# Other places in the steps for parts of a chunk's fronts and ends, in a two-layer kernel (selective scan, then outlook attention)

## The chip, the cores and the metric

The kernel runs on one core of a Trainium2 chip. What is measured is the device time of one execution in microseconds. Five engines work side by side, each through its own instruction stream in order: TensorE (PE; its weight loads are listed as PEld), VectorE (DVE), ScalarE (ACT), GpSimd (POOL), and SyncE (SP), which here only issues transfers (DMAs).

## The reference, cut to what matters

Input `x` has shape (4, 384, 64, 64); all data are float32. Two residual layers follow each other, each on a group norm of its input. The change concerns the first, a selective state-space layer over L = 4096 positions with 768 inner channels and 16 states:

```python
xn = (xs - mu) * jax.lax.rsqrt(var + 1e-05) * ln_w + ln_b
xz = jnp.einsum('blc,dc->bld', xn, in_proj_w)
xb, z = jnp.split(xz, 2, axis=-1)
xc = _silu(conv(xb, conv_w) + conv_b)            # 4 taps, one filter per channel
x_dbl = jnp.einsum('bld,ed->ble', xc, x_proj_w)  # 24 columns dt, 16 B, 16 C
dt = softplus(jnp.einsum('blr,dr->bld', dt, dt_w) + dt_b)
def step(h, inp):
    dA = jnp.exp(dt_t[:, :, None] * A[None])
    h = dA * h + (dt_t * x_t)[:, :, None] * B_t[:, None, :]
    y_t = jnp.einsum('bdn,bn->bd', h, C_t)
y = (ys + xc * D) * _silu(z)
out = jnp.einsum('bld,cd->blc', y, out_proj_w)
```

(The convolution's call and the loop over positions are shortened here.) The second layer, an outlook attention with 3 x 3 windows, is not touched.

## The kernel before, in words

**Tiling.** The 4096 positions of each of the four images are cut into 17 chunks of TM = 241, so there are 68 chunks. A chunk's scan takes NU = 12 steps; a step is one "unit" of 64 channels with all 16 states, which are laid on partitions and in four groups. The loop at line 805 runs over steps `s`; `s` modulo 12 is the place of a step in the chunk that is being scanned.

**The scan of a unit** is spread over several steps. `s_inputs` (line 625, POOL) and `s_inputs2` (line 640, DVE) multiply `dxr` with B into a buffer `h`, half of the groups each; `s_decay` (line 649, ACT) computes exp(dt A) into `da` in PSUM, four instructions for each half unit; `s_scan` (line 661, DVE) does the recurrence, twice per unit; `s_outputs` (line 671, POOL) multiplies by C; `s_sum` (line 676, PE), at odd steps, adds the states of two units up into `y`; `s_gate` (line 694, DVE) applies the gate. `h` has five buffers, so at an odd step the buffer for unit `s + 2` is one that `s_sum` of the same step must have read.

**The fronts and ends.** What comes before a chunk's scan (load, layer norm, in-projection, convolution, silu, the projections to dt, B and C, softplus, and the stores of dt x and dt to DRAM from where they are fetched back in the scan's layout) and what comes after it (out-projection, residual, store) is cut into parts, `f_...` and `e_...`. The dictionaries `plan` (line 505) and `ends` (line 540) give each part a place: a relative step and one of six slots within it, EARLY, READY, SCAN, POOL, MID, LATE. `parts(s, when)` (line 567) runs those that fall due. Relative step `r` of a chunk `k` is `s - 12 (k - 2)`; the chunk's own scan begins at `r = 24`, so parts with `r` from 12 to 23 run beside the scan of the chunk before, at its steps `r - 12`. An end's key counts from 36 later. At one slot the newer chunk's parts come first. `catch_up` (line 556) maps the same table onto the few steps before the second chunk.

**What sets the order.** Every engine is wrapped in `InOrder` (line 34), so its instructions run in the order in which the Python code issues them. A step issues, in this order: fetches (even steps), EARLY, `s_inputs2`, `s_gate` (even steps), READY, the statistics of the next image's input where due, first scan, carry and first decay, save, second scan, SCAN, second decay, `s_outputs`, POOL, `s_inputs`, `s_sum` (odd steps), MID, LATE.

**Buffers.** All tiles `ps_...` of the fronts and ends (and `pm`, `pv`, `pb` of the group norm) share the pool `pmm` with two PSUM buffers: an engine that is to write a new one waits until the last reader of an older one is done. Which of the two is taken is settled when the program is built. `dtx` has two buffers in SBUF, `xr` two.

Parts that the text names: `f_square` (299), `f_pow` (321), `f_rs` (325), `f_scale` (336), `f_x` and `f_z` with `project` (347 to 398), `f_conv` (375), `f_silu` (406), `f_bc` (414), `f_xd` (424), `f_dt` (434), `f_log` (456), `f_spread` (462), `f_plog` (481), `f_dtx` (486), `e_load` (705), `e_project` (710), `e_store` (718).

Of the kernel before, what the change touches and what calls it, by code (L numbers as in the profile page):

```python
# [7 lines left out]
F32 = mybir.dt.float32  # L8
AF = mybir.ActivationFunctionType
# [3 lines left out]
P = 128  # L13
# [7 lines left out]
TM = 241  # L21
# [54 lines left out]
def group_norm_coeffs(pe, ve, ae, gp, small, psum, blk12, mhalf, st, sc, bi):  # L76

    mv = small.tile([P, NCB, 2], F32, tag="mv", name="mv")  # L80
    neg = small.tile([P, 1], F32, tag="mg", name="neg")
    dev = small.tile([P, NCB], F32, tag="dev", name="dev")
    for cb in range(NCB):
        ve.bn_aggr(mv[:, cb, :], st[cb])
    yield False
    ps = psum.tile([P, 2, TM], F32, tag="mm", name="pm")
    for cb in range(NCB):
        pe.matmul(ps[:, 0, 0:1], blk12, mv[:, cb, 0:1], start=(cb == 0), stop=(cb == NCB - 1))
    yield True
    ae.mul(neg, ps[:, 0, 0:1], -1.0)  # L90
    ae.activation(dev, mv[:, :, 0], AF.Square, bias=neg)
    yield False
    ps = psum.tile([P, 2, TM], F32, tag="mm", name="pv")
    for cb in range(NCB):
        pe.matmul(ps[:, 0, 0:1], blk12, mv[:, cb, 1:2], start=(cb == 0), stop=False)
    for cb in range(NCB):
        pe.matmul(ps[:, 0, 0:1], blk12, dev[:, cb : cb + 1], start=False, stop=(cb == NCB - 1))
    yield True
    ve.tensor_scalar_add(sc, ps[:, 0, 0:1], 1e-5)
    gp.tensor_tensor(sc, sc, mhalf[:, 0:1], ALU.pow)  # L100
    yield False
    ae.mul(bi, neg, sc)
# [3 lines left out]
def mamba_layer(ctx, tc, x, w, x1, sc1, bi1, consts, behind):  # L106
# [16 lines left out]
    blk12, ident, eps, one = consts  # L123
    pe, ve, ae, gp, sp = (
        InOrder(tc, e) for e in (nc.tensor, nc.vector, nc.scalar, nc.gpsimd, nc.sync)
    )
# [12 lines left out]
    pmm = ctx.enter_context(tc.tile_pool(name="pmm", bufs=2, space=bass.MemoryType.PSUM))  # L139
# [294 lines left out]
    def f_dt(c, jj):  # L434
        t = c.t
        if jj == 0:
            c.dt = front.tile([P, NJ, TM], F32, tag="dt", name="dt")
        pp = pmm.tile([P, 2, TM], F32, tag="mm", name="ps_dt")
        for h in range(2):
            j = 2 * jj + h  # L440
            pe.matmul(
                pp[:, h, :t], wdt[:, j * P : (j + 1) * P], xd[:, 1:], start=True, stop=True
            )
        ae.activation(c.dt[:, 2 * jj : 2 * jj + 2, :t], pp[:, :, :t], AF.Exp)

    def store(v, d):
        for q in range(4):
            sp.dma_start(d[:, :, q, :].rearrange("j c t -> c j t"), v[CG * q : CG * (q + 1)])
# [31 lines left out]

    def f_plog(c, jj):

        c.pl = pmm.tile([P, 2, TM], F32, tag="mm", name="ps_lg")
        ae.activation(c.pl, c.dt[:, 2 * jj : 2 * jj + 2, :], AF.Ln, bias=one)

    def f_dtx(c, jj):
        if jj == 0:
            c.dxd = dram.tile([NJ, CG, 4, TM], F32, tag="dxd", name="dxd")
        dtx = front.tile([P, 2, TM], F32, tag="dtx", name="dtx", bufs=2)
        ve.tensor_mul(dtx, c.pl, c.xc[:, 2 * jj : 2 * jj + 2, 1:])  # L490
        store(dtx, c.dxd[2 * jj : 2 * jj + 2])


# [2 lines left out]
    EARLY, READY, SCAN, POOL, MID, LATE = range(6)  # L496

    def at(f, *args):
        def part(c):
            f(c, *args)  # L500

        part.f = f
        return part
# [2 lines left out]
        (-12, SCAN): [f_load],  # L506
        (-10, EARLY): [f_mean],
        (-10, READY): [f_center],
        (-9, POOL): [f_square],
        (-7, EARLY): [f_var],  # L510
        (-7, MID): [f_root],
        (-6, SCAN): [f_pow],
        (-5, READY): [f_rs],
        (-5, SCAN): [f_scale],
        (6, MID): [at(f_x, 0)],
        (8, EARLY): [at(f_z, 0)],
        (8, MID): [at(f_x, 1)],
        (9, POOL): [at(f_z, 1)],
        (9, MID): [at(f_conv, 0)],
        (10, LATE): [at(f_z, 2)],  # L520
        (11, LATE): [at(f_x, 2)],
        (12, SCAN): [at(f_conv, 1)],
        (12, LATE): [at(f_conv, 2)],
        (13, POOL): [at(f_silu, "xc", "zs")],
        (14, POOL): [f_bc],
        (15, EARLY): [f_xd],
        (16, READY): [at(f_dt, 0)],
        (16, SCAN): [at(f_dt, 1)],
        (17, EARLY): [at(f_dt, 2)],
        (17, READY): [at(f_plog, 0)],  # L530
        (17, MID): [at(f_dtx, 0)],
        (18, EARLY): [at(f_plog, 1)],
        (18, SCAN): [at(f_dtx, 1), at(f_plog, 2)],
        (19, READY): [at(f_dtx, 2)],
        (19, POOL): [f_log],
        (19, MID): [f_spread],
        (22, SCAN): [f_b],
    }

# [2 lines left out]
        (4, READY): [lambda c: e_project(c, 0)],  # L542
        (6, EARLY): [lambda c: e_project(c, 1)],
        (6, POOL): [lambda c: e_project(c, 2)],
        (15, EARLY): [lambda c: e_store(c)],
    }

    def chunk(k):
# [152 lines left out]
    def e_tokens(c, v):  # L701

        return v[c.b, :, c.t0 - 1 + c.lo : c.t0 - 1 + TM].rearrange("(p cb) l -> p cb l", cb=NCB)
# [6 lines left out]
    def e_project(c, cb):  # L710
        lo = c.lo
        po = pmm.tile([P, 2, TM], F32, tag="mm", name="ps_out")
        pe.matmul(po[:, 0, lo:], ident, c.xr[:, cb, lo:TM], start=True, stop=False)
        for j in range(NJ):
            pe.matmul(po[:, 0, lo:], wout[:, j, cb, :], c.zs[:, j, lo:TM], start=False, stop=(j == NJ - 1))
        ae.copy(c.xr[:, cb, lo:TM], po[:, 0, lo:])

    def e_store(c):
        if c.ci == 0:
            st1[c.b] = small.tile([P, NCB, NC, 6], F32, tag="st1", name="st1")  # L720
        for cb in range(NCB):
            ve.bn_stats(st1[c.b][:, cb, c.ci, :], c.xr[:, cb, c.lo : TM])
        sp.dma_start(e_tokens(c, x1), c.xr[:, :, c.lo : TM])
        if c.ci == NC - 1:
            b = c.b
            st = [st1[b][:, cb].rearrange("p a s -> p (a s)") for cb in range(NCB)]
            made = group_norm_coeffs(
                pe, ve, ae, gp, small, pmm, blk12, mhalf, st, sc1[:, b : b + 1], bi1[:, b : b + 1]
            )
            norms.append([made, False])  # L730
# [509 lines left out]
def layers(ctx, tc, w, out):  # L1240
# [26 lines left out]

    started = []
    mamba_layer(tc, x.rearrange("b c h w -> b c (h w)"), w, x1, sc1, bi1, consts, behind)
    outlook_layer(tc, x1, w, out, sc1, bi1, weights, ready)  # L1270

# [68 lines left out]
```

## Time and profile before

| | |
|---|---|
| time, median of 3 runs | 6282.82 us (6279.14 to 6284.06) |
| the profiled execution's own time | 6275.31 us |
| its span, first to last instruction | 6273.5 us |
| granted TensorE clock, mean | 0.94 |
| busy: PE, DVE, ACT, POOL | 88%, 86%, 74%, 85% of the span |
| first layer's scans | about 115 to 5036 us of the span |

The page cuts the span into 40 slices of about 157 us; slices 2 to 32 are the first layer, the rest the second. A row of the groups gives line, engine, operation, what is written from what, shapes and count, then busy time in us and mean ns of one, then the engine's idle time just before and what ended it. Nearly every instruction has line 49, that of the helper which keeps the order, so groups are told apart by the names of their tiles. In the timeline a row is start and length in us, engine and instruction, and in brackets the idle time before it with its releaser. A wait for several things is put down to the one that came last.

### The profile page before, as it was taken

How to read it: one execution, taken by the hardware profiler on the slowest of the kernel's cores; microseconds unless marked ns; L12 is line 12 of the kernel's file. 1: busy time of each engine (PE TensorE's matmuls, PEld its weight loads, DVE VectorE, ACT ScalarE, POOL GpSimd, SP SyncE). 2: the span in 40 equal slices, each digit the busy share in tenths (PEclk: the TensorE clock that was granted, in tenths of full speed). 3: DMA queues.
4: the chain of work that ended last, by engine and by line, in shares of the span. 5: the costliest groups of instructions: out<-in, count | busy, mean ns of one | idle time of the engine just before them, and what ended most of it. 6: DMA issues, size and time to landing. Idle time of an engine off the chain costs nothing. (4 is left out here: it accounts for less than half of the span.)

```text
span 6273.5 us, 114492 instructions
## 1 busy us (share of the span) xinstructions
PE 5513.1 (88%) x40506; PEld 4095.6 (65%) x40506; DVE 5373.4 (86%) x4786; ACT 4673.2 (74%) x11842; POOL 5307.6 (85%) x2047
## 2 busy tenths in 40 slices
PE   6888888888888888888888888888888789999999
PEld 5666666666666666666666666666666555555555
DVE  4999999999999999999999999999999955445444
ACT  3788888888888888888888888888888745444544
POOL 3999999999999999999999999999999944433333
PEclk9999999999999999999999999999999899999999
DMA  4555555545555555555555545545545644454544
GB/s 133 130 137 142 146 140 129 136 131 141 147 140 133 142 132 143 141 133 132 142 138 143 140 132 133 133 130 141 137 125 133 169 149 162 166 171 165 173 169 147
DMA packets 649765, 894.95 MB, mean 143 GB/s; under 512 B 138964, under 2 KB 543846, under 8 KB 649062
## 3 DMA queue, kind: packets, MB, share of 16 engines
q1 hardware_dynamic: 649190, 887.63, 51.0%
q8 instruction: 319, 5.23, 0.4%
q14 instruction: 256, 2.10, 0.1%
HBM read 661.53 MB, written 225.70 MB: 141 GB/s over the span
## 5 line engine op out<-in xcount | busy, mean ns | idle before, releaser
L49 DVE TENSOR_TENSOR_SCAN h<-da,h 128x968 f32<-128x968 f32 x1632 | 3452.0, 2158 | 30.4 <-POOL h L49 22.9
L49 POOL TENSOR_TENSOR h<-h,bc 128x1928 f32<-128x1928 f32 x816 | 3229.1, 3957 | 8.9 <-DVE h L49 8.9
L49 ACT ACTIVATE da<-dtr,aneg 128x241 f32<-128x241 f32 x6528 | 2642.1, 451 | 428.5 <-DVE h L49 403.8
L49 POOL TENSOR_TENSOR h<-dxr,bc 128x964 f32<-128x964 f32 x816 | 1627.7, 1995 | 116.5 <-PE y L49 96.8
L49 PE MATMUL ps_in<-u,win 128*128 128x241 f32 x4896 | 1119.2, 384 | 134.5 <-ACT xr L49 123.7
L49 PEld LDWEIGHTS ps_in<-u,win 128*128 128x128 f32 x4896 | 944.2, 197 | 298.5 <-ACT xr L49 148.2
L49 POOL TENSOR_TENSOR bd<-ain,own 99x1188 f32<-99x1188 f32 x192 | 413.4, 2181 | 726.5 <-DMA ain<-ad 557.5
L49 DVE TENSOR_TENSOR h<-dxr,bp 128x964 f32<-128x964 f32 x816 | 930.4, 1140 | 103.7 <-PE y L49 93.8
L49 PE MATMUL y<-h,ssum 128*32 128x241 f32 x13056 | 860.4, 385 | 52.8 <-POOL h L49 52.5
L49 PEld LDWEIGHTS y<-h,ssum 128*32 128x32 f32 x13056 | 422.5, 114 | 438.2 <-issue 166.1
L49 PE MATMUL ps_cv<-xb,cdiag 128*128 128x241 f32 x3264 | 693.9, 368 | 3.5 <-ACT neg L49 3.3
L49 PEld LDWEIGHTS ps_cv<-xb,cdiag 128*128 128x128 f32 x3264 | 611.1, 189 | 75.8 <-issue 25.1
L49 PE MATMUL psv<-wv,xp 128*128 128x384 f32 x1728 | 592.3, 494 | 7.9 <-issue 7.9
L49 PE MATMUL ps_xd<-xc,wx 128*128 128x241 f32 x816 | 328.9, 588 | 288.8 <-ACT xc L49 288.8
L49 PE MATMUL ps_out<-zs,wout 128*128 128x241 f32 (+1 forms) x2448 | 537.7, 369 | 0.0
L49 ACT ACTIVATE bd<-ain,own 99x324 f32<-99x324 f32 x704 | 334.7, 556 | 262.5 <-PE ps L49 243.8
L49 DVE TENSOR_TENSOR fold<-fold,ps 128x192 f32<-128x192 f32 (+1 forms) x768 | 211.3, 303 | 331.5 <-PE ps L49 317.1
L49 PEld LDWEIGHTS ps_out<-zs,wout 128*128 128x128 f32 x2448 | 469.0, 192 | 36.1
L49 PEld LDWEIGHTS ps_xd<-xc,wx 128*128 128x128 f32 x816 | 250.4, 316 | 355.6 <-ACT xc L49 314.2
L49 PEld LDWEIGHTS psv<-wv,xp 128*128 128x128 f32 x1728 | 322.4, 191 | 232.8 <-issue 19.9
L49 ACT COPY vst<-psv 128x384 f32<-128x384 f32 x279 | 131.1, 471 | 323.1 <-PE psv L49 323.1
L49 PE MATMUL ps_dt<-xd,wdt 128*128 128x241 f32 x816 | 243.2, 426 | 84.9 <-ACT dt L49 79.7
(108 smaller groups left out, 5461.6 us busy)
## 6 DMA issues: line engine op xcount, KB each, us to landing
dxr<-dxd SPq DMA_DIRECT2D x1632, 120.5 KB
dtr<-dtd SPq DMA_DIRECT2D x1632, 120.5 KB
bc<-bcd SPq DMA_DIRECT2D x544, 120.5 KB
vin<-vd SPq DMA_DIRECT2D x384, 148.5 KB
vd<-vst SPq DMA_DIRECT2D x93, 576.0 KB
dxd<-dtx SPq DMA_DIRECT2D x816, 60.2 KB
dtd<-dt SPq DMA_DIRECT2D x272, 180.8 KB
xs<-in_x SPq DMA_DIRECT2D x96, 256.0 KB
```

Of the source, the lines that this page charges most:

```text
L49: made = self.tc.keep_in_program_order(issue(*args, **kwargs))
```

## The change

Ten entries of the two tables get other places, and the tile that `f_plog` hands to `f_dtx` is kept per index in a dictionary instead of in one attribute.

```diff
@@ f_dt
         if jj == 0:
             c.dt = front.tile([P, NJ, TM], F32, tag="dt", name="dt")
+            c.pl = {}
@@ f_plog, f_dtx
-        c.pl = pmm.tile([P, 2, TM], F32, tag="mm", name="ps_lg")
-        ae.activation(c.pl, c.dt[:, 2 * jj : 2 * jj + 2, :], AF.Ln, bias=one)
+        c.pl[jj] = pmm.tile([P, 2, TM], F32, tag="mm", name="ps_lg")
+        ae.activation(c.pl[jj], c.dt[:, 2 * jj : 2 * jj + 2, :], AF.Ln, bias=one)
...
-        ve.tensor_mul(dtx, c.pl, c.xc[:, 2 * jj : 2 * jj + 2, 1:])
+        ve.tensor_mul(dtx, c.pl[jj], c.xc[:, 2 * jj : 2 * jj + 2, 1:])
@@ plan
-        (-9, POOL): [f_square],
+        (-9, LATE): [f_square],
...
-        (-6, SCAN): [f_pow],
+        (-6, LATE): [f_pow],
...
-        (6, MID): [at(f_x, 0)],
+        (6, LATE): [at(f_x, 0)],
...
-        (9, MID): [at(f_conv, 0)],
+        (9, LATE): [at(f_conv, 0)],
...
-        (12, SCAN): [at(f_conv, 1)],
-        (12, LATE): [at(f_conv, 2)],
+        (12, MID): [at(f_conv, 1)],
+        (13, SCAN): [at(f_conv, 2)],
...
         (16, SCAN): [at(f_dt, 1)],
-        (17, EARLY): [at(f_dt, 2)],
+        (16, MID): [at(f_dt, 2)],
         (17, READY): [at(f_plog, 0)],
...
-        (19, READY): [at(f_dtx, 2)],
-        (19, POOL): [f_log],
-        (19, MID): [f_spread],
+        (19, EARLY): [at(f_dtx, 2)],
+        (19, MID): [f_log, f_spread],
@@ ends
-        (15, EARLY): [lambda c: e_store(c)],
+        (14, POOL): [lambda c: e_store(c)],
```

## The prediction

> **What bounds the kernel now.** I read the page first (slices and groups), then the waits of 1000 to 4600 us, where nothing but the first layer runs, then one chunk instruction by instruction in the timeline. "Step m" is the place 0 to 11 of a scan step in its chunk.
>
> ```profile
> span 6273.5 us, 114492 instructions
> ...
> DVE  4999999999999999999999999999999955445444
> ...
> POOL 3999999999999999999999999999999944433333
> ...
> L49 POOL TENSOR_TENSOR h<-h,bc 128x1928 f32<-128x1928 f32 x816 | 3229.1, 3957 | 8.9 <-DVE h L49 8.9
> ...
> L49 POOL TENSOR_TENSOR h<-dxr,bc 128x964 f32<-128x964 f32 x816 | 1627.7, 1995 | 116.5 <-PE y L49 96.8
> ```
>
> Two engines are at nine tenths for the whole first layer. POOL's two multiplies start 5.85 us apart per step in the timeline (they overlap a little); with the power's 0.66 us a chunk cannot be shorter than 12 x 5.85 + 0.66 = 70.86 us. The first scans of the second and of the 67th chunk start at 203.13 and 4893.38 us (VectorE's timeline): 65 chunks at 72.16 us. So at most 65 x 1.30 = 85 us is to be had. What ends last in a chunk?
>
> ```profile
> PE ps_in L49 <- ACT xr L49: 95.1, 50, 2.2
> ...
> DVE h L49 <- PE y L49: 63.8, 57, 1.4
> POOL h L49 <- PE y L49: 61.4, 37, 4.4
> ...
> DVE u L49 <- PE ps_rs L49: 39.0, 25, 2.7
> ```
>
> These are waits over 50 chunks. Each chunk has a DVE wait of 1.21 us for PE's sum, half of them one of up to 1.7 us for `ps_rs`, and all 50 have PE waiting for an `xr` copy ahead of `ps_in`. The timeline shows it as one chain at steps 6 to 8 (ScalarE, TensorE, VectorE):
>
> ```profile
> 2483.79 0.67 ACT L49 ACTIVATE ps_lg<-dt,one 128x482 f32<-128x482 f32 x1 [0.80 <-DVE dtx L49]
> 2484.40 1.60 ACT L49 ACTIVATE da<-dtr,aneg 128x241 f32<-128x241 f32 x4
> 2485.94 0.35 ACT L49 COPY xr<-ps_out 128x241 f32<-128x241 f32 x1
> ```
> ```profile
> 2486.35 2.71 PE L49 MATMUL ps_in<-u,win 128*128 128x241 f32 x12 [1.92 <-ACT xr L49]
> ...
> 2489.85 1.84 PE L49 MATMUL y<-h,ssum 128*32 128x241 f32 x32
> ```
> ```profile
> 2484.74 0.65 DVE L49 TENSOR_TENSOR dtx<-ps_lg,xc 128x482 f32<-128x482 f32 x1
> ...
> 2491.72 1.16 DVE L49 TENSOR_TENSOR h<-dxr,bp 128x964 f32<-128x964 f32 x1 [1.21 <-PE y L49]
> ```
>
> After scan 6 the second `dtx` (0.64) frees a PSUM buffer; the third `ps_lg` (0.67), four exponentials (1.60) and the `xr` copy (0.35) follow on ACT; only then is there a buffer for the projection `x0` (to `ps_rs` 2.55), then `ps_rs` and the sum (2.8), 8.6 us in all. DVE's own work beside it is 7.4, so it waits 1.21. A chunk without input statistics: 69.01 of DVE work + 1.21 + 0.61 (step 3, below) = 70.83, as the timeline has it; with them 70.22 + 1.21 = 71.43. And in about half of the chunks `x0` itself is slow:
>
> ```profile
> 4219.65 4.40 PE L49 MATMUL ps_in<-u,win 128*128 128x241 f32 x12 [1.92 <-ACT xr L49]
> ```
>
> 4.40 instead of 2.71: 1.68 us more, which DVE waits out at `ps_rs`.
>
> **What the Trainium skill says.** "TensorE: Matmul & The Clock Gate", Part 1: the array's clock falls to half after an idle window of about 3.4 us, the windows run free, and speed returns after a busy one. The trace agrees in kind, by 4.40 against 2.71 for the same twelve matmuls, but here 1.92 us of waiting and shorter waits before it are enough, and it hits about every second chunk. The same page, "Architectural detail", says that ScalarE, VectorE and GpSimd queues are strictly first in, first out: the `xr` copy, ready at 2484.43, stands behind the exponentials until 2485.94.
>
> **The change part by part.** Ten entries move. Four cross nothing on their engines: `f_square`, `f_x` 0, `f_conv` 0 and `f_log` (between old and new slot ACT, PE and SP issue nothing else at those steps). Cost 0. `c.pl` as a dictionary issues nothing. Those that cross something:
>
> 1. `f_conv` 1 and 2. PE's order stays. On ACT, conv 1's two evacuations (0.69 from start to start) go behind four exponentials, where ACT has waits; conv 2's go between the pairs of exponentials of step 1. There ACT waits only 0.31 us for a scan:
>
> ```profile
> 2453.16 1.62 ACT L49 ACTIVATE da<-dtr,aneg 128x241 f32<-128x241 f32 x4 [0.31 <-DVE h L49]
> ```
> so this start, the silu, its two table loads and the exponentials of step 2 move by 0.69 - 0.35 = 0.34 us. DVE waits for the last at step 3:
> ```profile
> 2462.11 4.24 DVE L49 TENSOR_TENSOR_SCAN h<-da,h 128x968 f32<-128x968 f32 x2 [0.61 <-POOL h L49]
> ```
> (POOL's product was ready long before; the exponentials end at 2462.03.) So +0.34 per chunk on DVE; where statistics (0.60) fill the wait, +0.34 too.
>
> 2. `f_dt` 2 ahead of `f_var`. ACT's order stays. `ps_dt` 2 (0.92) no longer waits for `dt` 1, the variance does (its wait becomes some 0.8). The sum behind starts within 0.2 us of before; POOL needs it 2.5 us later. 0, between -0.3 and +0.2.
>
> 3. `f_pow` behind two POOL multiplies instead of ahead. Those run 0.66 earlier, nobody waits for them. The power ends at 2487.9 instead of 2482.1; `ps_rs` started at 2488.9. Cover 1.0 us: 0 as things stand, 0.2 if PE comes at 2487.75 (below).
>
> 4. `e_store`. The statistics keep their place in DVE's order. SP issues the output store ahead of the `bcd` stores; SP idles there from 2451.8 to 2464.2. The `xr` load, which waited 2.9 us for that store to land, and the fetches, the statistics load and the `dtx` stores behind it come up to 3.5 us sooner. No steady-state wait on a DMA is seen, so 0 by itself.
>
> 5. `f_dtx` 2 ahead of `s_inputs2` at step 7. It needs the third `ps_lg`, which needs the second `dtx`: DVE stops 0.80 us (ACT 2483.79 to 2484.46, 2484.5 against 2483.69). The multiply and scan 7 behind it come 0.85 later, inside the 1.21 that DVE waits at step 8 anyway. In return `dtx` 2 ends at 2485.1, and with it the second PSUM buffer is free 1.2 us before the `xr` copy (2486.29).
>
> **Where I choose.** Two PSUM buffers serve all these tiles, and which one `x0` gets is fixed when the program is built. Before, `dtx` 2 ended at 2485.39 and still `x0` waited for the `xr` copy of 2486.29. With `dtx` 2 first on DVE and its stores' queue 3 us earlier, I take it that `x0` gets the buffer of `dtx` 2. The profile doesn't show this; it is the main doubt. Bounds for it: 0, and what follows.
>
> Then `x0` runs 2485.2 to 2487.75, `ps_rs` after the power (2487.95), the sum to 2490.8; DVE reaches step 8 at 2491.2 with no wait, in place of 2491.72. PE's wait before `x0` falls from 1.92 to 0.8, and I take the slow `x0` to go. Chunk without statistics: 69.01 + 0.95 + 0.80 = 70.76, so POOL's 70.86; with: 70.22 + 0.35 + 0.80 = 71.37. About 36 of 65 chunks' worth have statistics: mean 71.14; chunks that form coefficients keep their extra (some 0.19 on the mean, from three of about +2.7 and six of +0.7): 71.33. 72.16 - 71.33 = 0.83, x 65 = 54 us. The profiled execution took 6275.3 (span 6273.5 and 1.8 around), 7.5 under the median; so 6282.8 - 54, about **6229**. Late next: POOL itself.
>
> **The rivals.**
> - *Buffer unchanged, lateness hidden.* `x0` goes on waiting for `xr`. Moves 3 to 5 sink in the 1.21; the 0.34 is mostly lost in the pattern of fast and slow `x0`, of which a shifted chunk may have fewer or more. For it: before, the earlier release wasn't used. Against: both things that `dtx` 2 hangs on come sooner. 6283, within 12.
> - *Slower: conv 2's evacuations.* With the buffer unchanged, the 0.34 us at step 3 stays in line with the 1.21 at step 8, for all 65 chunks: +22, **6305**. It decides as soon as the evacuations (0.69) exceed ACT's waits ahead of the silu (0.31 here) and no POOL wait absorbs it; POOL has gaps of 0.6 in chunks with statistics, so they take DVE's pace. Against: POOL-paced chunks hide it.
> - *The power holds `ps_rs`.* If POOL runs a microsecond later against DVE, the sum comes as late as before and the 1.21 returns: only the slow `x0` (56.5 us of waits in the whole profile, part of it start-up) would shrink. About 6255; inside the forecast's range.
>
> **How the numbers follow.** Forecast 0.57 (of which 0.12 is the power's case), unchanged 0.20, slower 0.23. The forecast's own range is 6198 (POOL's floor, 85 us) to 6262. For 8 in 10, with cases of both signs, the range runs from 6192 (the floor, and a few us of start-up, whose order moves too) to 6306. 0.2% is 12.6 us, about what this kernel's measurement resolves. Faster: 0.57 + a fifth of 0.20 = 0.61; slower: 0.23 less what comes out under 12 us, plus a little of the unchanged case, 0.22; the same 0.17.
>
> **What would show it.** `ps_in` waiting for `dtx` instead of `xr`, some 0.8 us each; DVE waits for `ps_lg` of 0.8 per chunk; `u<-u` waits on `ps_rs` gone; DVE's wait at step 3 at 0.95; POOL waits for `y` near 0.6 or none. I am wrong if `ps_in` still waits for ACT `xr` near 1.9.

## The result, and the profile after

The changed kernel takes 6228.76 us (median of 4 runs, 6226.16 to 6232.5) beside 6282.69 us for the kernel before on the same chip: ratio 0.9915, 95% interval 0.9898 to 0.9933. 6229 was predicted.

First the page of the changed kernel (group rows: busy us, mean ns of one, idle us before and its main releaser):

```profile
span 6224.4 us, 114423 instructions
...
L49 PE MATMUL ps_in<-u,win 128*128 128x241 f32 x4896 | 1073.5, 373 | 45.0 <-DVE dtx L49 33.5
...
L49 PE MATMUL ps_out<-zs,wout 128*128 128x241 f32 (+1 forms) x2448 | 592.0, 396 | 0.0
```

The same two rows of the kernel before:

```profile
L49 PE MATMUL ps_in<-u,win 128*128 128x241 f32 x4896 | 1119.2, 384 | 134.5 <-ACT xr L49 123.7
...
L49 PE MATMUL ps_out<-zs,wout 128*128 128x241 f32 (+1 forms) x2448 | 537.7, 369 | 0.0
```

Then the changed kernel's waits of 1000 to 4600 us (total, times, longest):

```profile
DVE dtx L49 <- ACT ps_lg L49: 61.7, 50, 1.8
...
PE ps_in L49 <- DVE dtx L49: 16.6, 20, 0.9
```

`ps_in` waits for the reader of the other buffer, `dtx`, and no longer for the `xr` copy: 134.5 us of idle time before `ps_in` have become 45.0, and its mean has gone from 384 to 373 ns. In exchange VectorE now waits for `ps_lg` in every chunk. The row to stop at is that of `ps_out`: the change doesn't touch it, and its mean went from 369 to 396 ns.

The period of a chunk is read from VectorE's timeline, first scan of the second to first scan of the 67th chunk: 72.16 before, 71.49 now. Over those 65 chunks VectorE's gaps of more than 0.15 us add up, by step of the chunk, to:

| VectorE waits, us in 65 chunks | before | after |
|---|---|---|
| step 3, for the exponentials | 18.4 | 35.8 |
| step 7, `dtx` for `ps_lg` | 1.6 | 79.7 |
| step 8, for `ps_rs` | 50.9 | 0 |
| step 8, for `y` | 78.9 | 2.2 |

That is 32 us less. The span has 49 less, of which 44 lie in these chunks. All of VectorE's gaps in these chunks, short ones too, give 35 of the 44. The other 9 are no gaps: from one start to the next, gaps left out, VectorE's instructions take 4534.1 us before and 4525.4 now. Of this 6.5 is the multiply that reads `ps_rs` (0.97 each before, 0.87 now): it overlaps its follower by some 0.1 us where the follower needn't wait.

What makes the 79.7 is seen in one chunk of the changed kernel, in the timeline of TensorE, ScalarE and VectorE:

```profile
2454.74 0.68 PE L49 MATMUL ps_out<-xr,ident 128*128 128x241 f32 x2 [1.92 <-DVE dtx L49]
2455.25 4.11 PE L49 MATMUL ps_out<-zs,wout 128*128 128x241 f32 x12
...
2460.32 2.61 PE L49 MATMUL ps_out<-zs,wout 128*128 128x241 f32 x12
2462.90 2.69 PE L49 MATMUL ps_in<-u,win 128*128 128x241 f32 x12
```
```profile
2459.40 0.36 ACT L49 COPY xr<-ps_out 128x241 f32<-128x241 f32 x1 [3.09 <-PE ps_out L49]
...
2461.41 0.66 ACT L49 ACTIVATE ps_lg<-dt,one 128x482 f32<-128x482 f32 x1
```
```profile
2462.09 0.66 DVE L49 TENSOR_TENSOR dtx<-ps_lg,xc 128x482 f32<-128x482 f32 x1 [1.33 <-ACT ps_lg L49]
2462.67 1.15 DVE L49 TENSOR_TENSOR h<-dxr,bp 128x964 f32<-128x964 f32 x1
```

`x0` runs at its fast 2.69 right behind the out-projections. But the out-projection at 2455.25 takes 4.11 where the next one, the same twelve matmuls, takes 2.61. ScalarE has to copy its result before it comes to the exponentials and the third `ps_lg`, and VectorE, which now reads that `ps_lg` at once, waits 1.33 instead of 0.73. Over the 65 chunks the two go together without exception: this projection takes over 3.5 us in 38 of them, and in these the wait is over 1.2 us; in the other 27 it is 0.73 or 0.74. The slow stretch of the matmuls has moved from `x0`, slow in 29 of 65 chunks before and in none now, to the projection before it, slow in 4 before and in 38 now.

### The profile page after: what moved, and what is told of

It is laid out like the page before. It is cut to its first block, busy times and chain, and to the rows that moved or that the text cites. A ratio compares the mean times of both kernels' runs of the same rounds, so it can differ in the third digit from the quotient of the medians.

```text
span 6224.4 us, 114423 instructions
## 1 busy us (share of the span) xinstructions
PE 5485.2 (88%) x40506; PEld 4055.1 (65%) x40506; DVE 5363.2 (86%) x4786; ACT 4667.1 (75%) x11842; POOL 5307.3 (85%) x2047
## 5 line engine op out<-in xcount | busy, mean ns | idle before, releaser
L49 PE MATMUL ps_in<-u,win 128*128 128x241 f32 x4896 | 1073.5, 373 | 45.0 <-DVE dtx L49 33.5
L49 PEld LDWEIGHTS ps_in<-u,win 128*128 128x128 f32 x4896 | 910.9, 190 | 202.3 <-ACT zs L49 32.8
L49 PE MATMUL ps_xd<-xc,wx 128*128 128x241 f32 x816 | 309.0, 558 | 323.9 <-ACT xc L49 323.9
L49 PE MATMUL ps_out<-zs,wout 128*128 128x241 f32 (+1 forms) x2448 | 592.0, 396 | 0.0
L49 PEld LDWEIGHTS ps_out<-zs,wout 128*128 128x128 f32 x2448 | 510.2, 208 | 50.7
L49 PE MATMUL ps_dt<-xd,wdt 128*128 128x241 f32 x816 | 205.9, 389 | 71.7 <-ACT dt L49 64.6
```

Source lines behind the costliest of these rows:

```text
L49: made = self.tc.keep_in_program_order(issue(*args, **kwargs))
```

## The experiments

The kernel before ran beside all twelve kernels below at 6279.5 to 6279.8 us; on that scale the changed kernel is at 6226 (0.9915 x 6279.7). Two theories were set against each other: A, that the gain comes from the buffer that `x0` gets; B, that it comes from the new places themselves.

**Only the buffer, and everything but the buffer.** For these the pool's choice was replaced by one written out: two tags of one buffer each, used in turn, except where `same` keeps the last one. (The class around `tile` and the line that makes the pool are left out here.)

```diff
+    def tile(self, shape, dtype, tag, name, same=False):
+        self.n += not same
+        return self.pool.tile(shape, dtype, tag=f"mm{self.n % 2}", name=name)
...
-        c.pl = pmm.tile([P, 2, TM], F32, tag="mm", name="ps_lg")
+        c.pl = pmm.tile([P, 2, TM], F32, tag="mm", name="ps_lg", same=jj == 0)
```

This is b_x0. In a_x0 the order is that of the changed kernel and `same` stands at `x0` (`name="ps_in", same=jj == 0`) instead of at `ps_lg`.

> The order of the kernel before in every engine; only the PSUM buffer of x0 (first in-projection) is changed: it takes the one of the third ps_lg, which the second dtx frees, and ps_rs takes the one that the xr copy frees. Theory A (the gain of the change comes from this buffer): x0 waits for DVE dtx and no longer for ACT xr, starts about 0.9 us sooner, the DVE wait for y at step 8 falls from 1.21 to about 0.3, and the chunks come near POOL's floor of 70.9: 6205 to 6240 us, as fast as the changed kernel or faster. Theory B (the gain comes from the new places themselves, above all dtx 2 ahead of the DVE multiply): the same as before, 6283 within 12.

> The order of the changed kernel in every engine; only x0 takes the PSUM buffer that the xr copy frees, as before the change. Theory A: the wait of ps_in for ACT xr comes back (some 1.9 us in every chunk), and with conv's evacuations in the silu chain (0.3 per chunk) it is no faster than the kernel before: 6275 to 6305. Theory B: it stays at the changed kernel's time, 6229 within 12.

Measured: b_x0 6191.66 us, ratio 0.9861 (0.9846 to 0.9875); a_x0 6285.97 us, ratio 1.0011 (1.0000 to 1.0022). b_x0 is below the range that was expected of it, a_x0 within its own. The timelines of TensorE and VectorE in b_x0, in the same steps as above:

```profile
1660.79 2.61 PE L49 MATMUL ps_out<-zs,wout 128*128 128x241 f32 x12
1664.42 2.72 PE L49 MATMUL ps_in<-u,win 128*128 128x241 f32 x12 [1.02 <-DVE dtx L49]
1666.98 0.60 PE L49 MATMUL ps_rs<-ident,vs 121*128 121x121 f32 x4
```
```profile
1663.72 0.65 DVE L49 TENSOR_TENSOR dtx<-ps_lg,xc 128x482 f32<-128x482 f32 x1
1664.29 4.23 DVE L49 TENSOR_TENSOR_SCAN h<-da,h 128x968 f32<-128x968 f32 x2
1668.43 0.94 DVE L49 SCALAR_TENSOR_TENSOR u<-u,bc,ps_rs 128x723 f32<-128x723 f32 x1
1669.80 1.16 DVE L49 TENSOR_TENSOR h<-dxr,bp 128x964 f32<-128x964 f32 x1 [0.43 <-PE y L49]
```

Without one instruction at another place, `x0` starts when `dtx` is done (1664.4), the wait for `y` falls from 1.21 to 0.43, no chunk waits for `ps_rs`, and the third `ps_lg` is there (1663.43) 0.28 us before VectorE comes to it. Over the 65 chunks VectorE's waits at step 8 fall from 129.8 to 30.4 us. About half of this is the shorter wait for `y` (78.9 to 30.4), and the other half, 50.9, is the wait for `ps_rs`: `x0` is slow in no chunk here. In a_x0 the old waits are back (1000 to 4600 us):

```profile
PE ps_in L49 <- ACT xr L49: 73.7, 50, 1.9
...
DVE dtx L49 <- ACT ps_lg L49: 57.8, 50, 1.8
...
DVE h L49 <- PE y L49: 35.2, 48, 1.4
```

So A holds, and more than that: the buffer by itself is worth 88 us, and the change as a whole gains 53. The new places as they stand cost about 35 us once the buffer is right (6191.7 to 6226). Which ones?

**`dtx` 2, alone and taken back.** b_dtx is the kernel before with this entry moved; the pool's own choice leaves `x0` with the `xr` buffer. a_nodtx is the changed kernel with it moved back; `x0` keeps the buffer of the third `ps_lg`. b_x0_dtx is b_x0 with it moved.

```diff
-        (19, READY): [at(f_dtx, 2)],
+        (19, EARLY): [at(f_dtx, 2)],
```

> The kernel before with one entry moved, dtx 2 from READY to EARLY of step 19; the buffers come out as in the kernel before (x0 takes the one of the xr copy). Theory A: no gain, 6283 within 12 (DVE stops about 0.8 for the third ps_lg at step 7 and waits as much less at step 8). Theory B: most of the gain, 6230 to 6250.

> The changed kernel with dtx 2 back behind the DVE multiply (19 READY); x0 stays in the third ps_lg's buffer. If the early place only costs (DVE stops 0.73 for the third ps_lg and gains about 0.43 at step 8 by it): 6205 to 6215. If the early place brings the gain by freeing the buffer sooner: 6240 to 6255.

> b_x0 with dtx 2 ahead of the DVE multiply as in the change. If its early place only costs: DVE stops about 0.73 for the third ps_lg in every chunk and saves the 0.43 at step 8, +0.3 x 65 = 20 us, 6205 to 6215. If it helps: below 6190.

Measured: b_dtx 6282.86 us, ratio 1.0002 (0.9994 to 1.0011); a_nodtx 6212.00, ratio 0.9894 (0.9879 to 0.9909); b_x0_dtx 6208.42, ratio 0.9885 (0.9870 to 0.9900). Alone it does nothing: what VectorE waits more at step 7 it waits less at step 8. With the right buffer its early place costs about 17 us (6208.4 less 6191.7), or 14 when counted from the other side (6226 less 6212.0). In both pairs the intervals overlap a little, so the sizes are rough, but both go the same way. In VectorE's gaps of the 65 chunks, steps 7 and 8 together hold 60.6 us in a_nodtx (16.9 for `ps_lg`, 43.7 for `y`) and 81.9 in the changed kernel. The later place puts the 1.15 us multiply into the time in which ScalarE is still at `ps_lg`.

**The convolution's evacuations.** a_noconv is the changed kernel with these two taken back.

```diff
-        (12, MID): [at(f_conv, 1)],
-        (13, SCAN): [at(f_conv, 2)],
+        (12, SCAN): [at(f_conv, 1)],
+        (12, LATE): [at(f_conv, 2)],
```

> The changed kernel with conv 1 and conv 2 at their old places (12 SCAN, 12 LATE). The buffers stay as in the changed kernel. If the evacuations delay the silu chain by 0.29 us per chunk as the step 3 waits say (65 chunks, 19 us), it is about 6210; if the slack is taken up elsewhere (POOL's floor), 6220 to 6229; if the new places help in another way, slower than 6235.

Measured: 6214.56 us, ratio 0.9895 (0.9878 to 0.9911), about 12 us less than the changed kernel; the intervals of the two overlap, so the size is rough. The direction is plain in VectorE's timeline at step 3 of a chunk without statistics, the changed kernel first, then a_noconv:

```profile
2439.12 4.24 DVE L49 TENSOR_TENSOR_SCAN h<-da,h 128x968 f32<-128x968 f32 x2 [0.89 <-POOL h L49]
```
```profile
2434.93 4.24 DVE L49 TENSOR_TENSOR_SCAN h<-da,h 128x968 f32<-128x968 f32 x2 [0.61 <-POOL h L49]
```

Summed over 65 chunks this wait is 35.8 us against 18.7: 17 us of waits for about 12 us of time.

**`dt` 2 and the store: what turns the pool's choice, and the slow projection.** Read in the programs as built: `dt` 2 alone gives `x0` the better buffer in the chunks without statistics only, the store alone in none, both together in all. The two together were run, neither of them alone with the pool's own choice:

```diff
-        (17, EARLY): [at(f_dt, 2)],
+        (16, MID): [at(f_dt, 2)],
...
-        (15, EARLY): [lambda c: e_store(c)],
+        (14, POOL): [lambda c: e_store(c)],
```

b_dt2_store is the kernel before with these two. b_x0_dt2 has `dt` 2 alone with buffers by hand, b_x0_dt2alt the same with the buffers in plain alternation, and a_x_nodt2 is the changed kernel with `dt` 2 back at its place and the buffers by hand as in b_x0. Theory S says that the earlier `dt` 2 makes TensorE wait longer ahead of the second out-projection, and that this wait makes the projection slow.

> The kernel before with two entries moved as in the change, dt 2 (16 MID) and the end's store (14 POOL), nothing set by hand. In the program as built x0 now takes the buffer of the third ps_lg; either of the two entries alone doesn't do that in all chunks, and dtx 2 alone (b_dtx) in none. Theory A: ps_in waits for DVE dtx, most of the gain or more than it comes with these two, 6192 (b_x0) to 6225. If the other eight entries carry the gain: near 6280.

> b_x0 (order of the kernel before, x0 in the third ps_lg's buffer) with dt 2 ahead of the variance as in the change. Theory S (the earlier sum lengthens PE's wait before the second out-projection from about 0.75 to 1.92, and that makes this projection slow in about half of the chunks): ps_out goes from 371 to 385-396 ns in the mean, and the time from 6192 to 6205-6218. If the slow ps_out comes from another entry: ps_out stays at 371 ns, 6192 within 8.

> The changed kernel with dt 2 back at its old place (17 EARLY), x0 kept by hand in the third ps_lg's buffer. Theory S: ps_out falls from 396 to about 370 ns, DVE's waits for the third ps_lg are 0.73 in every chunk with none of 1.3 to 1.8, and the time falls by some 0.8 us in 55% of 65 chunks, 29 us, to about 6200. If the slow ps_out has another cause: 6229 within 8.

> The order of the kernel before with dt 2 ahead of the variance, and the two buffers in plain alternation (b_x0_dt2 had put the first ps_lg into the buffer that the variance holds until DVE has read it, which cost 3.1 us of ACT in every chunk; here it takes that of the third ps_dt, as in the changed kernel). Theory S: ps_out near 386 ns as in b_dt2_store, time 6192 to 6202.

Measured: b_dt2_store 6196.28 us, ratio 0.9869 (0.9854 to 0.9884). Two of the ten entries give 83 us. b_x0_dt2 missed at 6254.18, ratio 0.9960 (0.9946 to 0.9975), because it changed a second thing: with `dt` 2 ahead of the variance, "the last buffer" at the first `ps_lg` was the variance's. One line of its waits (1000 to 4600 us) says it:

```profile
ACT ps_lg L49 <- DVE vs L49: 156.9, 50, 3.2
```

ScalarE stood 3.1 us in each of the 50 chunks for VectorE to read the variance: another wrong buffer, and 58 us lost to it. With that mended, b_x0_dt2alt takes 6196.33, ratio 0.9867 (0.9853 to 0.9882): the same as b_dt2_store, so the store's place is worth nothing beyond the choice that it turns.

The slow projection does come with `dt` 2. Rows of the pages of b_x0, b_dt2_store and a_x_nodt2, in this order:

```profile
L49 PE MATMUL ps_out<-zs,wout 128*128 128x241 f32 (+1 forms) x2448 | 542.5, 371 | 0.0
```
```profile
L49 PE MATMUL ps_out<-zs,wout 128*128 128x241 f32 (+1 forms) x2448 | 572.0, 386 | 0.0
```
```profile
L49 PE MATMUL ps_out<-zs,wout 128*128 128x241 f32 (+1 forms) x2448 | 550.9, 375 | 0.0
```

371 ns without the move, 386 with it, and 375 where it is taken out of the changed kernel (396). In b_x0_dt2alt, which moves `dt` 2 and not the store, it is 388. Counted by chunks, the second out-projection is slow in 8 of 65 in b_x0 and 28 in b_x0_dt2alt, in 38 in the changed kernel and 15 in a_x_nodt2. What this costs depends on what stands behind: with `dtx` 2 at its old place at most some 5 us (6196.3 against 6191.7, within the intervals). a_x_nodt2 took 6216.60 us, ratio 0.9903 (0.9887 to 0.9920): about 10 us off the changed kernel, with intervals that overlap, and not the 29 expected. Its 65 chunks still hold 15 long waits for `ps_lg` (38 in the changed kernel), one for each slow projection. One of them in TensorE's timeline:

```profile
1733.45 1.17 PE L49 MATMUL ps_out<-xr,ident 128*128 128x241 f32 x2 [2.38 <-DVE dtx L49]
1734.42 3.69 PE L49 MATMUL ps_out<-zs,wout 128*128 128x241 f32 x12
```

There the work ahead was done early too, and the wait for `dtx` was 2.38. But in the same run other projections are fast behind waits of up to 2.38. So S is right that moving `dt` 2 makes this projection slow more often; that the length of the wait does it is not shown. In size S was too large by a factor of about three.

**A version of its own.** If the sum is late because `x0` stands ahead of it, `x0` can go behind it.

```diff
-        (6, MID): [at(f_x, 0)],
+        (7, MID): [at(f_x, 0)],
```

b_late is the kernel before with this entry; b_late_hand adds the buffers by hand as in b_x0, so that `ps_rs` gets the third `ps_lg`'s.

> The kernel before with one entry moved that the change leaves alone in substance: x0 goes behind the sum of step 7 (7 MID instead of 6 MID). In the program as built ps_rs takes the buffer that the xr copy frees. If the chain behind that copy costs only because the 2.55 us of x0 stand in it: ps_rs and the sum start at the copy, DVE's waits for y and ps_rs at step 8 go altogether (1.21 per chunk and the slow x0), and the time is 6165 to 6195, as good as b_x0 or better. If x0's later place is paid back (ACT's xb copy, the convolution, the silu at step 3 later): 6200 to 6260.

> b_late with ps_rs by hand in the third ps_lg's buffer and x0 in the one of the xr copy. If b_late still waits for the copy, this is faster by up to 0.4 per chunk (27 us) than it; if DVE's own work is the bound by then, the same within 6.

Measured: b_late 6218.66 us, ratio 0.9900 (0.9884 to 0.9917), over 20 us above what was expected of the first case and inside the range of the second; b_late_hand 6186.16, ratio 0.9850 (0.9835 to 0.9864), the lowest of all medians and 32 us below b_late, where up to 27 was expected. b_late's TensorE:

```profile
1742.30 0.68 PE L49 MATMUL ps_rs<-ident,vs 121*128 121x121 f32 x4 [2.01 <-ACT xr L49]
1742.81 0.97 PE L49 MATMUL y<-xc,ddiag 128*128 128x241 f32 x2
1743.72 3.07 PE L49 MATMUL y<-h,ssum 128*32 128x241 f32 x32
```

The expectation left no room for a slow sum. Behind the wait for `xr`, now 2.01 us, it takes 3.07 instead of 1.84, and VectorE waits 0.57 for it at step 8; the in-projections behind it are late too, and two waits of 0.32 at steps 9 and 10 follow. Over the 65 chunks VectorE's gaps at steps 8, 9 and 10 are 27, 31 and 19 us. In b_late_hand, where `x0` stands at the same late place, they are 1, 7 and 3, so it is the wait for `xr` that costs, and not the place. Here the sum is what comes next after that wait, and it takes over 2.3 us in 48 of 64 chunks; in the kernel before it was `x0`, slow in 29 of 65. In b_late_hand the wait is for `dtx` (about 1.1 us, the sum over 2.3 in 25 of 64), and the period is 70.82 us, at POOL's floor of the prediction (70.86). POOL's pace in that run is still about 5.85 a step, and its waits for `y` between 1000 and 4600 us come to 4.6 us, 61.4 in the kernel before.

```profile
1690.00 4.12 POOL L49 TENSOR_TENSOR h<-h,bc 128x1928 f32<-128x1928 f32 x1
...
1695.86 4.11 POOL L49 TENSOR_TENSOR h<-h,bc 128x1928 f32<-128x1928 f32 x1
...
1701.69 4.13 POOL L49 TENSOR_TENSOR h<-h,bc 128x1928 f32<-128x1928 f32 x1
```

## Why the prediction was right, and where it was not

- **The choice of the buffer**, named as the main doubt, is what the gain hangs on; b_x0 and a_x0 show it from both sides. The reason given for it was wrong in the main. "With `dtx` 2 first on DVE and its stores' queue 3 us earlier" names `dtx` 2, which has no part in it: b_dtx moves it and the buffer stays, a_nodtx takes it back and the buffer stays. The other half of the sentence comes from the output store's new place, and this has a part, but only together with `dt` 2, which had been put down at 0. So it was partly luck that the right buffer came out, though what it does was read rightly.
- **Item 5**, `dtx` 2. "Inside the 1.21 that DVE waits at step 8 anyway" is right with the old buffer (b_dtx, 1.0002). In the forecast's own case the 1.21 no longer exists: with the right buffer and `dtx` 2 at its old place only 0.43 is left of it. The early place is paid with 0.73 to save 0.43. I counted the 0.80 in the forecast, but as the price of the gain, and it is none: 14 to 17 us were given away there.
- **Item 1**, the evacuations: +0.34 at step 3 was forecast, 0.28 is in the timeline (0.61 to 0.89). The rival that made them the whole story would have been a_x0, new order with the old buffer: 6286, not 6305.
- **Item 2** failed: "0, between -0.3 and +0.2". I looked at ScalarE's order and at the sum, not at what comes behind it on TensorE: the wait for `dtx` ahead of the out-projection (0.75 in the prediction's chunk, 1.92 in the changed kernel's chunk above), and that projection, which is slow in more chunks with the move (28 against 8, 38 against 15).
- **"I take the slow `x0` to go"**: it went, and reappeared one tile earlier. Steps 7 and 8 were to hold about 52 us of VectorE's waits in 65 chunks (0.80 each) and held 82. That is the term that was too small.
- **Item 4**, 0 for the store by itself, stands (b_x0_dt2alt and b_dt2_store agree). **The power** never held `ps_rs` back in the chunk shown: it ends at 2464.1 and `ps_rs` starts at 2465.4. Over the chunks of the first layer `ps_rs` waits for it four times, 0.47 us at most. `f_pow`, `f_square`, `f_x` 0, `f_conv` 0 and `f_log` were not tried alone; 12 us for the convolution, 14 to 17 for `dtx` 2 and 5 to 10 for `dt` 2 leave little of the 35 for them, but each of these differences is uncertain by some 10 us, and they needn't add up.
- **The sum.** A mean period of 71.33 was forecast, 71.49 measured, 10 us more over 65 chunks. The hit on 6229 is partly luck: about 5 us came off before and after those chunks, which was not in the sum, and the profiled execution is 2.6 us faster than the median (it was 7.4 before).

POOL's floor was a sound bound for the mean (70.82 in b_late_hand, where POOL hardly waits); single chunks can be shorter (70.01 in b_late_hand) while POOL falls behind VectorE.

## What to carry to other kernels

Where tiles share a small pool, ask for each tile which earlier reader frees its buffer, and look at that assignment again after every edit: two moves that had been put at nothing turned it, and one buffer was worth more (88 us) than the ten moved entries together (53). Write such an assignment out by hand when a wait hangs on it. And where the profile has slow stretches behind TensorE's waits, ask of each move which work comes next behind such a wait, and what it costs if that work runs at its slow time.

## What was not expected of the hardware

The Trainium skill ("TensorE: Matmul & The Clock Gate", Part 1) puts the fall of TensorE's clock to half at an idle window of about 3.4 us. Here less is enough: single waits of 1.92 to 2.38 us are followed by stretches 1.4 to 1.7 times as long (4.11 and 3.69 against 2.61, 3.07 against 1.84). That it is the clock stands in the trace: in the chunk of the changed kernel above, the granted clock is 1.00 from 2450 to 2455 us, 0.50 from 2457 to 2459 and 1.00 from 2461 to 2465. The wait alone doesn't decide: in b_x0 an out-projection ran fast behind nearly the same wait.

```profile
1656.71 0.68 PE L49 MATMUL ps_out<-xr,ident 128*128 128x241 f32 x2 [1.87 <-DVE dtx L49]
1657.22 2.61 PE L49 MATMUL ps_out<-zs,wout 128*128 128x241 f32 x12
```

In the changed kernel, too, slow projections stand behind waits of 0.70 to 2.89 us and fast ones behind 0 to 1.92. The page also says that the windows run free, and the trace agrees: all changes of the granted clock in the first layer lie on one grid of 3.41 us. But what in a window makes the next one slow stays open. In the changed kernel TensorE was idle for as little as 0.18 of a window after which the clock fell, and for up to 0.52 of one after which it stayed full (with matmul ends as the profile models them).
